# A preLN graph layer on one Trainium2 core: 46 chunks of edges taken as columns out of a table in SBUF, in place of 18 chunks loaded by single rows

## The chip, the core and the metric

The kernel runs on one core of one Trainium2 chip. The metric is the device time in microseconds (us) of one execution. Of the core's engines, TensorE (PE in the profile) does the matrix products and the transposes, VectorE (DVE) the elementwise work on masks and means, ScalarE (ACT) the activations and the copies out of PSUM, GpSimd (POOL) issues the indirect gathers, and SyncE (SP) issues the other DMAs of the main loop. Each engine works through its own list of instructions in order, and waits on semaphores for the others.

## The reference

12,500 nodes with 128 features, and 200,000 edges sorted by their target `dst`. What is computed:

```python
h = jnp.maximum(_layernorm(x, axis=-1), 0.0)
msgs = h[src]
agg = jax.ops.segment_sum(msgs, dst, num_segments=n)
deg = jax.ops.segment_sum(jnp.ones(E), dst, num_segments=n)
agg = agg / jnp.maximum(deg, 1.0)[:, None]
h0 = jax.nn.relu(agg @ Wg + h @ Ws + bg)      # 128 -> 128
h1 = jnp.tanh(h0 @ W1 + b1)                   # 128 -> 512
h2 = jnp.tanh(h1 @ W2 + b2)                   # 512 -> 512
out = x + h2 @ W3 + b3                        # 512 -> 128
```

Everything is float32.

## The kernel before

**Stage one** normalizes x in pieces of up to 14 tiles of 128 rows (L225 to L243), and stores the result h as a table `htab` of 512-byte rows in HBM. The same stage loads `src` and `dst`, turns them with PE, and keeps them as one column per chunk (`scol`, `dloc`).

**The edges** are cut into 1563 chunks of 128. A chunk needs a tile `rows` with 128 rows of h, one per edge, on 128 partitions. A one-hot mask `oh` (edges by target nodes of a window of 144) stands on the other side, and one matmul, `rows` as weights and the mask as moving data, adds the chunk's messages to `agg` in PSUM, features on partitions (`add`, L418). There are three ways to get the rows:

- 80 "raw" chunks (10 groups of 8, one group every 40 chunks from chunk 256) are gathered from x itself during stage one, by POOL (L147), and normalized in the main loop.
- 18 "slow" chunks (from chunk 160 on, every 73rd that is not raw; L96 to L104) are loaded by `row_loads` (L321) on SP's queue: 32 row numbers at a time go from SBUF into registers (a TENSOR_LOAD, L327), and each row is then a DMA of its own, whose address is a register.
- The other 1465 are gathered by POOL with one indirect DMA each (`gather`, L312). `rows_in` has `AHEAD` = 40 buffers, so the gather of a chunk waits for the matmul of the chunk 40 gathers earlier.

**The nodes** are cut into blocks of 512 (23 of them, then smaller ones). When the chunks of a block are done, the layers follow: `mean` (DVE), `part0` to `part4` (matmuls with an activation on ACT after each). These are generators; up to chunk 1312 (`QUICK`) the loop takes one step of them every second chunk, so that PE does layers between chunks, and from chunk 1312 on a small planner in the loop (`there`, `go_on`) decides. `part0` needs h of the block's own nodes, turned: `own` (L473) loads four tiles of `htab` into `hb`, `own_turned` (L482) transposes them on PE into `pt`, and ACT copies them to `hT`, one block of 512 every 64 chunks.

**Order.** The instructions of PE, the activations and copies on ACT that go through the class `act`, and the DMAs of `sp_dma` are kept in program order. The rest is placed by the framework's scheduler. `onehot(g + 2)` (L363) writes the mask of a group of 8 chunks two groups ahead, into one of `OHS` = 4 buffers.

Of the kernel before, what the change touches and what calls it, by code (L numbers as in the profile page):

```python
# [31 lines left out]
P = 128  # L32
EPS = 1e-5
CPR = 16
BLK = 512
PIECE = 14
GRP = 8
NRAW = 10
RAW0 = 256
STEP = 40  # L40
AHEAD = 40
LATE = 12
LEAD = 16
QUICK = 1312
SLOW0 = 160
EACH = 72
TOGETHER = 4
# [12 lines left out]
def windowed(ctx, tc, x, src, dst, Wg, Ws, bg, W1, b1, W2, b2, W3, b3, out, flag):  # L60
# [34 lines left out]

    slow, n = [], 0  # L96
    for c in range(SLOW0, NCH - 12):
        if raw(c):
            continue
        if n <= 0:  # L100
            slow.append(c)
            n = EACH
        else:
            n -= 1  # L104

# [11 lines left out]
    rows_in = ctx.enter_context(tc.tile_pool(name="rows_in", bufs=AHEAD))  # L117
    rows_one = ctx.enter_context(tc.tile_pool(name="rows_one", bufs=4))
    ps_c = ctx.enter_context(tc.tile_pool(name="ps_c", bufs=1, space=PSUM))
# [46 lines left out]

    htab = dram.tile([NP, D], F32, name="htab")
    scol = const.tile([P, NCOL], I32, name="scol")
    dloc = const.tile([P, NCOL], F32, name="dloc")

# [5 lines left out]
    def centre(pool, xt, k, stats, bufs=2):  # L176
        nc.vector.tensor_reduce(stats[:, 0], xt, AX.X, ALU.add)  # L177
        nc.vector.scalar_tensor_tensor(xt, spread(stats[:, 0], k), -1.0 / D, xt, op0=ALU.mult, op1=ALU.add)
        sq = pool.tile([P, k, D], F32, name=f"sq{k}", bufs=bufs)
# [13 lines left out]
    with tc.tile_pool(name="setup", bufs=1) as sp, tc.tile_pool(name="ln", bufs=2) as ln:  # L193

        def indices(name, a, pad, keep):
            r = sp.tile([NROW, ROW], I32, name="idx_raw")

            nc.vector.memset(r, pad)
            even = FULL // 16 * 16
            for s0, s1 in ((0, even), (even, FULL)):  # L200
                if s1 > s0:
                    nc.scalar.dma_start(r[s0:s1, :], a[s0 * ROW : s1 * ROW].rearrange("(p e) -> p e", e=ROW))
            nc.scalar.dma_start(r[FULL : FULL + 1, :REST], a[FULL * ROW : E].rearrange("(p e) -> p e", p=1))
            rf = sp.tile([NROW, ROW], F32, name="idx_f")
# [21 lines left out]
        for i, (t0, k) in enumerate(pieces):  # L226
# [13 lines left out]
            factors(stats)  # L240
            h = ln.tile([P, PIECE, D], F32, name="h")
# [40 lines left out]
    nc.scalar.dma_start(b3c, b3.rearrange("(p o) -> p o", o=1))  # L282
    ROWB = 4 * D
    hbytes = htab.rearrange("n d -> (n d)").bitcast(U8)
    at_i = const.tile([len(slow), P], I32, name="at_i")
# [34 lines left out]

    def row_loads():  # L321
        for i, c in enumerate(slow):
            r = rows_one.tile([P, D], F32, name="srows")
            rows_t[c] = r
            rb = r.bitcast(U8)
            for p0 in range(0, P, LOADS):
                loads, vs = nc.values_load_multi_w_load_instructions(  # L327
                    place[i : i + 1, p0 : p0 + LOADS], engines=[mybir.EngineType.SP], min_val=0,
                    max_val=(N - 1) * ROWB,
                    skip_runtime_bounds_check_because="src holds rows of x, as the indirect DMAs take it to",  # L330
                )
                for ld in loads:
                    tc.keep_in_program_order(ld)
                for p, v in enumerate(vs, p0):
                    sp_dma(rb[p : p + 1, :], hbytes[bass.ds(v, ROWB)].rearrange("(o b) -> o b", o=1))
                    if (p + 1) % TOGETHER == 0:
                        yield


# [18 lines left out]

    OHS = 4
    oh_bufs = [const.tile([P, GRP, WINDOWS[0][1]], F32, name=f"oh{i}") for i in range(OHS)]  # L360
    counts = {}

    def onehot(g):  # L363
        k = min(GRP, NCH - g * GRP)
        lo, w = window(g * GRP)
        is_raw = raw(g * GRP)
        oh = ed.tile([P, GRP, W_RAW], F32, name="ohr", bufs=2) if is_raw else oh_bufs[g % OHS]
        nc.vector.tensor_tensor(  # L368
# [28 lines left out]
    def count(b):  # L397

        n, m = blocks[b]
        dg = flat(ps_m.tile([P, 4, P], F32, name="pm"))  # L400
        pe.matmul(dg[:, :m], ones, counts.pop(b)[:, :m], start=True, stop=True)
        rd = ml.tile([P, BLK], F32, name="rd", bufs=3)
# [67 lines left out]

    owns, hTs, xss, stores = {}, {}, {}, []

    def own(s):  # L473

        n0 = s * BLK
        n = min(BLK, N - n0)
        k = -(-n // P)
        hb = ml.tile([P, BLK // P, D], F32, name="hb", bufs=3)
        sp_dma(hb[:, :k], htab[n0 : n0 + k * P, :].rearrange("(t p) d -> p t d", p=P))
        owns[s] = hb  # L480

    def own_turned(s):  # L482

        k = -(-min(BLK, N - s * BLK) // P)
        hb = owns.pop(s)
        pt = ps_t.tile([P, BLK // P, P], F32, name="pt")
        for t in range(k):
            pe.transpose(pt[:, t, :], hb[:, t, :], ident)
        hT = ml.tile([P, BLK], F32, name="hT", bufs=3)
        act.copy(hT[:, : k * P], pt[:, :k, :].rearrange("p t n -> p (t n)"))  # L490
        hTs[s] = hT

# [26 lines left out]
    def mean(b):  # L519
        n, mm, hop = costs(b)  # L520
        yield 0, 0
        mTs[b] = ml.tile([P, BLK], F32, name="mT")
        merged(b, mTs[b])

    def part0(b):
        n, mm, hop = costs(b)
        s, off = divmod(blocks[b][0], BLK)
        yield mm, 0
        p0 = flat(ps_m.tile([P, 4, P], F32, name="pm"))
        pe.matmul(p0[:, :n], ws, hTs[s][:, off : off + n], start=True, stop=False)  # L530
        yield mm, n / 90
        pe.matmul(p0[:, :n], wg, mTs.pop(b)[:, :n], start=False, stop=True)
        h0s[b] = ml.tile([P, BLK], F32, name="h0")
        act.activation(h0s[b][:, :n], p0[:, :n], AF.Relu, bias=bgc)
# [75 lines left out]

    order = [c for c in range(NCH) if not raw(c) and c not in slow]
    loading = row_loads()
    work, done, nxt, behind = [], 0, 0, 0
    ngrp = -(-NCH // GRP)
    span = BLK // per
    now = at = 0
# [9 lines left out]
    def go_on(w):  # L626
        nonlocal now
        if w:
# [3 lines left out]
            if w[1] is None:  # L632
                work.remove(w)

    own(0)
    own(1)
    own(2)
    own_turned(0)
    onehot(0)
    onehot(1)  # L640
    counted = 0
    for c in range(NCH):
# [3 lines left out]
        if c % GRP == 0 and g + 2 < ngrp:  # L646
            onehot(g + 2)
            if raw((g + 2) * GRP):
                raw_scaled(((g + 2) * GRP - RAW0) // STEP)
            if 2 <= g < 2 + NRAW:  # L650
# [10 lines left out]
        if not raw(c) and c not in slow:  # L661
            behind += 1
            batch = behind * P // (EACH * TOGETHER)
            if behind > SLOW0 - 3 * EACH and batch > (behind - 1) * P // (EACH * TOGETHER):
                next(loading, 0)
        if c >= QUICK:

            there = 7.5 + 1.251 * (NRAW * GRP + order.index(c)) if c not in slow else 0
            while soonest() and max(now, soonest()[2]) < there:
# [403 lines left out]
```

## Time and profile before

| | |
|---|---|
| median of 3 runs | 1958.97 us (1958.91 to 1960.45) |
| time of the profiled execution | 1958.05 us |
| its span, first to last instruction | 1954.9 us |
| granted TensorE clock, mean | 0.895 |
| busy: PE, DVE, ACT, POOL | 1361.4, 1108.8, 219.0, 1465.8 us |
| indirect DMAs on POOL | 80 from x, 1465 from `htab` |
| rows as single DMAs on SP's queue | 2304 (18 x 128) |

How to read it: a line of a view names the line of the kernel, the engine, the operation, what it writes and reads (out<-in), the count, the busy time with the mean of one, and the idle time of the engine just before, with what ended it. "issue" is idle time in which the engine waited for nothing that the profile shows. SPq, ACTq and POOLq are an engine's sequencer: DMAs that it issues, register instructions and waits. These don't count as busy. A line like "x24" in the timeline is a run of 24 records of one group. An fp32 matmul leaves two records, so one chunk is two.

### The profile page before, as it was taken

The page shows a single profiled execution, that of the slowest core. Times are in us where ns is not written, and L with a number is a line of the kernel's source. Part 1 is how long each engine was busy: PE and PEld are TensorE (multiplying, and loading weights), DVE is VectorE, ACT ScalarE, POOL GpSimd, SP SyncE. Part 2 cuts the span into 40 slices and gives each one's busy share as a digit, 9 for nine tenths or more (in the row PEclk, how much of TensorE's full clock was granted, in tenths as well). Part 3 has the DMA queues.
Part 4 walks back from the last instruction along what each step waited for, and adds up shares of the span by engine and source line. Part 5 has one row for each costly group of instructions (what it writes and reads, how often), then busy time and mean ns, then how long its engine had stood idle before and what let it go on. Part 6 is the DMA issues. An engine that isn't in the chain of part 4 may idle for free.

```text
span 1954.9 us, 20999 instructions
## 1 busy us (share of the span) xinstructions
PE 1361.4 (70%) x4838; PEld 796.5 (41%) x4838; DVE 1108.8 (57%) x2650; ACT 219.0 (11%) x352; POOL 1465.8 (75%) x1553
## 2 busy tenths in 40 slices
PE   0056547777788877777766766766767678888797
PEld 0034334444444444444333333433333334454466
DVE  6874867548667667645456455454554544654541
ACT  1100010011111011101101011010110101011022
POOL 7777777777777777777777777777777777777775
PEclk9999958798989898987989989889899898788698
DMA  8822222222222222222222222222222223222221
GB/s 212 233 62 59 62 54 65 53 58 65 70 59 65 70 70 59 65 70 59 65 71 70 54 71 61 62 64 59 71 54 71 70 54 83 59 66 71 63 61 44
DMA packets 124143, 139.41 MB, mean 71 GB/s; under 512 B 32776, under 2 KB 98454, under 8 KB 123816
## 3 DMA queue, kind: packets, MB, share of 16 engines
q0 software_dynamic: 49440, 101.35, 20.6%
q1 hardware_dynamic: 71374, 33.32, 6.2%
q10 hardware_dynamic: 3196, 3.32, 0.7%
q8 instruction: 40, 0.66, 0.1%
q14 instruction: 93, 0.76, 0.1%
HBM read 125.06 MB, written 12.82 MB: 71 GB/s over the span
## 4 chain that ended last, share of the span: by engine, by line
DMA 30%; issue 29%; PE 28%; POOL 7%; DVE 5%; ACT 1%; SPq 0%; ACTq 0%; POOLq 0%; DVEq 0%
DMA rows<-htab,scol 27%; PE pm L301 16%; PE agg L301 9%; POOL rows L314 7%; PE edge L301 2%; DMA xt<-in_x_dram 2%; DVE deg L384 1%; PE pt L304 1%; DVE oh L368 1%; DMA at_i<-in_src_dram 0%; ACT h L344 0%; DVE h L191 0%; DVE agg L184 0%; DVE agg L177 0%; DVE sq L183 0%
## 5 line engine op out<-in xcount | busy, mean ns | idle before, releaser
L314 POOL DMA_INDIRECT rows<-htab,scol x1465 | 1388.2, 948 | 446.7 <-issue 272.3
L301 PE MATMUL agg<-oh,rows 128*128 128x144 f32 (+3 forms) x2098 | 551.6, 366 | 321.0 <-DMA rows<-htab,scol 292.7
L301 PEld LDWEIGHTS agg<-oh,rows 128*128 128x128 f32 x2098 | 392.1, 227 | 686.1 <-DMA rows<-htab,scol 527.2
L301 PE MATMUL pm<-h,w 128*128 128x512 f32 (+4 forms) x1344 | 653.8, 585 | 15.9 <-ACT h L344 15.8
L384 DVE SCALAR_TENSOR_TENSOR deg<-shared,dloc,deg 128x144 bf16<-128x144 f32 (+17 forms) x1921 | 567.0, 326 | 29.1
L368 DVE TENSOR_TENSOR oh<-shared,dloc 128x1152 f32<-128x1152 f32 (+2 forms) x186 | 245.5, 1320 | 446.1 <-PE agg L301 304.7
L301 PE MATMUL edge<-oh,rows 128*128 128x144 f32 (+2 forms) x832 | 215.1, 349 | 129.4 <-DMA rows<-htab,scol 129.1
L301 PEld LDWEIGHTS edge<-oh,rows 128*128 128x128 f32 x832 | 141.5, 208 | 286.5 <-DMA rows<-htab,scol 221.5
L301 PEld LDWEIGHTS pm<-h,w 128*128 128x128 f32 x1344 | 227.4, 209 | 34.0 <-ACT h L344 18.1
L344 ACT ACTIVATE h<-pm,b2c 128x512 f32<-128x512 f32 (+4 forms) x112 | 70.8, 632 | 678.9 <-PE pm L301 678.9
L403 DVE TENSOR_SCALAR rd<-pm 128x512 f32<-128x512 f32 (+4 forms) x28 | 17.4, 622 | 178.5 <-PE pm L301 178.5
L344 ACT ACTIVATE h<-pm,b1c 128x512 f32<-128x512 f32 (+4 forms) x112 | 70.4, 632 | 241.1 <-PE pm L301 240.5
L147 POOL DMA_INDIRECT raw<-in_x_dram,rsrc x80 | 76.7, 959 | 25.6 <-issue 23.8
L405 DVE RECIPROCAL rd<-rd 128x512 f32<-128x512 f32 (+4 forms) x28 | 81.8, 2920 | 0.0
L467 DVE TENSOR_TENSOR mT<-agg,sums 128x136 f32<-128x136 f32 (+6 forms) x57 | 15.3, 268 | 106.2 <-PE agg L301 105.5
L209 PE MATMUL pm<-ident,idx_f 98*128 98x98 f32 x32 | 6.0, 374 | 69.2 <-DVE idx_f L205 59.1
L347 ACT COPY hT<-pt 128x512 f32<-128x512 f32 (+1 forms) x25 | 14.4, 577 | 316.2 <-PE pt L304 304.3
L304 PE MATMUL pt<-ident,hb 128*128 128x128 f32 x98 | 17.3, 305 | 45.9 <-DMA hb<-htab 22.1
L344 ACT ACTIVATE h<-pm,bgc 128x512 f32<-128x512 f32 (+4 forms) x28 | 17.7, 632 | 158.5 <-PE pm L301 158.5
L209 PEld LDWEIGHTS pm<-ident,idx_f 98*128 98x128 f32 x32 | 5.1, 224 | 69.7 <-DVE idx_f L205 30.8
L304 PEld LDWEIGHTS pt<-ident,hb 128*128 128x128 f32 x98 | 13.0, 157 | 47.3 <-issue 47.3
L585 DVE TENSOR_TENSOR o<-pt,xb 128x512 f32<-128x512 f32 x23 | 15.5, 676 | 26.7 <-PE pt L304 26.6
(71 smaller groups left out, 468.5 us busy)
## 6 DMA issues: line engine op xcount, KB each, us to landing
srows<-htab SPq DMA_DIRECT2D x2304, 0.5 KB
rows<-htab,scol POOLq DMA_INDIRECT x1465
hb<-htab SPq DMA_DIRECT2D x24, 256.0 KB
xb<-in_x_dram SPq DMA_DIRECT2D x23, 256.0 KB
out_dram<-o SPq DMA_DIRECT2D x23, 256.0 KB
htab<-h SPq DMA_DIRECT2D x6, 896.0 KB
xt<-in_x_dram SPq DMA_DIRECT2D x5, 896.0 KB
raw<-in_x_dram,rsrc POOLq DMA_INDIRECT x80
```

Of the source, the lines that this page charges most:

```text
L147: nc.gpsimd.indirect_dma_start(out=t[:, j, :], out_offset=None, in_=x, in_offset=bass.IndirectOffsetOnAxis(ap=rsrc[:, g, j : j + 1], axis=0),)
L301: tc.keep_in_program_order(nc.tensor.matmul(*a, **k))
L304: tc.keep_in_program_order(nc.tensor.transpose(*a, **k))
L314: nc.gpsimd.indirect_dma_start(out=r, out_offset=None, in_=htab, in_offset=bass.IndirectOffsetOnAxis(ap=scol[:, c : c + 1], axis=0),)
L344: tc.keep_in_program_order(nc.scalar.activation(*a, **k))
L347: tc.keep_in_program_order(nc.scalar.copy(*a))
L368: nc.vector.tensor_tensor(oh[:, :k, :w], lane[:, None, :w].to_broadcast([P, k, w]), dloc[:, g * GRP : g * GRP + k][:, :, None].to_broadcas ...
L384: nc.vector.scalar_tensor_tensor(d, lane[:, a0 - lo : a1 - lo], dloc[:, c : c + 1], d, op0=ALU.is_equal, op1=ALU.add)
L403: nc.vector.tensor_scalar(rd[:, :m], dg[:, :m], 1.0, None, op0=ALU.max)
L405: nc.vector.reciprocal(rd[:, :m], rd[:, :m])
L467: nc.vector.tensor_tensor(out, s, t, op=ALU.add)
L585: nc.vector.tensor_tensor(o[:, :whole], po[:, :whole], xb[:, :whole], op=ALU.add)
```

## The change

A table `tab` of 128 partitions by 12,544 nodes (features on partitions, 50 KB on each) is kept in SBUF: `own_turned` now copies every turned block there, and all 25 blocks of `htab` are loaded and turned in the first 100 chunks, one every 4 chunks (before: one every 64). `part0` reads the block's own h from `tab`, and `hT` is gone.

46 chunks (the words of the change say 48; the rule in the code, with 152 candidates and three in ten, gives 46), between 155 and 1435, get their rows from `tab`: ACT loads 32 numbers into registers at a time, and copies for each edge the column of its source into a tile `cols` (128 partitions by 4 bytes per copy). `turn` transposes the 128 x 128 tile on PE into a `pm` buffer of PSUM, and ACT copies it to `turned`, from where `add` takes it. The copies are handed out in batches of four, `MARGIN` = 18 gathers ahead of the chunk's use, and spread evenly over the stretch from one such chunk to the next; `turn` comes 9 gathers ahead.

No chunk is loaded by single rows any more (`lanes[0]` is empty), nor by DVE (`lanes[2]`). The 18 small DMAs of `at_i` on ACT's queue are gone; two tiles `places` are made of the loaded `src` by DVE instead.

To make room: `AHEAD` 40 to 22, pieces of stage one of up to 11 tiles in place of 14, three mask buffers in place of four, one `ohr`, `mT` and `h0` in place of two, two `rd` in place of three, and `hb` shares the two buffers of `xb`.

```diff
-PIECE = 14
+PIECE = 11
-AHEAD = 40
+AHEAD = 22
-SLOW0 = 160
-EACH = 72
+EVERY = 8
+AT = 3
+LANES = "A--A--A---"
+FROM, UNTIL = 152, 1450
+SBUFS = 4
+MARGIN = 18
...
+    lanes = ([], [], [])
+    for i, c in enumerate(c for c in range(AT, NCH, EVERY) if FROM <= c < UNTIL and not raw(c)):
+        kind = LANES[i % len(LANES)]
+        if kind != "-":
+            lanes["SAV".index(kind)].append(c)
+    apart = sum(lanes, [])
...
+    tab = const.tile([P, NP], F32, name="tab")
+    places = [const.tile([NROW, CPR // EVERY, P], I32, name=f"place{i}") for i in range(2)]
...
+            if name == "src":
+                some = r.rearrange("r (q p) -> r q p", p=P)[:, AT::EVERY]
+                for to, step in zip(places, (ROWB, 4)):
+                    nc.vector.tensor_scalar(to, some, float(step), None, op0=ALU.mult)
...
-    for i, c in enumerate(slow):
-        nc.scalar.dma_start(at_i[i : i + 1, :], src[c * P : (c + 1) * P].rearrange("(o p) -> o p", o=1))
-    place = const.tile([len(slow), P], I32, name="place")
-    nc.vector.tensor_scalar(place, at_i, float(ROWB), None, op0=ALU.mult)
+    tbytes = tab.bitcast(U8)
...
+    def offsets(lane, c, p0):
+        step = ROWB if lane == 0 else 4
+        r, q = divmod(c, CPR)
+        kind = (mybir.EngineType.SP, mybir.EngineType.Activation, mybir.EngineType.DVE)[lane]
+        loads, vs = nc.values_load_multi_w_load_instructions(
+            places[min(lane, 1)][r : r + 1, q // EVERY, p0 : p0 + LOADS], engines=[kind], min_val=0, max_val=(N - 1) * step,
...
+    def column_copies(lane):
+        copy = nc.scalar.copy if lane == 1 else nc.vector.tensor_copy
+        for c in lanes[lane]:
+            t = ed.tile([P, P], F32, name=f"cols{lane}", bufs=2)
+            columns[c] = t
+            tb = t.bitcast(U8)
+            for p0 in range(0, P, LOADS):
+                for p, v in offsets(lane, c, p0):
+                    tc.keep_in_program_order(copy(tb[:, 4 * p : 4 * p + 4], tbytes[:, bass.ds(v, 4)]))
+                    if (p + 1) % (TOGETHER if lane == 1 else LOADS) == 0:
+                        yield
+
+    def turn(c):
+        pt = ps_m.tile([P, 4, P], F32, name="pm")
+        pe.transpose(pt[:, 0, :], columns.pop(c), ident)
+        r = ed.tile([P, D], F32, name="turned", bufs=3)
+        act.copy(r, pt[:, 0, :])
+        rows_t[c] = r
...
-    OHS = 4
+    OHS = 3
...
-        hb = ml.tile([P, BLK // P, D], F32, name="hb", bufs=3)
+        hb = ml.tile([P, BLK // P, D], F32, name="xb")
...
-        hT = ml.tile([P, BLK], F32, name="hT", bufs=3)
-        act.copy(hT[:, : k * P], pt[:, :k, :].rearrange("p t n -> p (t n)"))
+        act.copy(tab[:, s * BLK : s * BLK + k * P], pt[:, :k, :].rearrange("p t n -> p (t n)"))
...
+    def load_times(lane):
+        use = [sum(o < c for o in order) for c in lanes[lane]]
...
+        step = (use[-1] - use[0]) // max(1, len(use) - 1)
+        use = [max(FROM - 46 + MARGIN, use[0] - step), *use] if lane else [use[0] - step * k for k in range(SBUFS - 1, 0, -1)] + use
+        some = LOADS if lane == 2 else TOGETHER
+        for i in range(len(lanes[lane])):
+            for k in range(P // some):
+                yield max(1, use[i] + (use[i + 1] - use[i]) * k * some // P - (0, MARGIN, MARGIN + GRP)[lane])
...
+    turns = sorted((max(1, sum(o < c for o in order) - MARGIN // 2), c) for c in sum(lanes[1:], []))
...
+            for rows_of_lane, times in loading[:2]:
+                while times and times[0] <= behind:
+                    times.pop(0)
+                    next(rows_of_lane, 0)
+            while turns and turns[0][0] <= behind:
+                turn(turns.pop(0)[1])
...
-        if c % span == span // 2 and (c // span + 1) * BLK < N:
-            own_turned(c // span + 1)
-            if (c // span + 3) * BLK < N:
-                own(c // span + 3)
+        if c % 4 == 2 and c // 4 + 1 < nown:
+            own_turned(c // 4 + 1)
+            if c // 4 + 3 < nown:
+                own(c // 4 + 3)
```

More of the change, by code (lines that the diff above doesn't have):

```diff
@@ L94, in window @@
         return per * c + first(w), w
[L96 to L104, printed above, removed]
+    lanes = ([], [], [])
[4 more added lines that the diff above has]
+    apart = sum(lanes, [])
     blocks, n = [], 0
@@ L117, in windowed @@
     rows_in = ctx.enter_context(tc.tile_pool(name="rows_in", bufs=AHEAD))
-    rows_one = ctx.enter_context(tc.tile_pool(name="rows_one", bufs=4))
+    rows_one = ctx.enter_context(tc.tile_pool(name="rows_one", bufs=SBUFS))
     ps_c = ctx.enter_context(tc.tile_pool(name="ps_c", bufs=1, space=PSUM))
@@ L167, in windowed @@
     htab = dram.tile([NP, D], F32, name="htab")
+    tab = const.tile([P, NP], F32, name="tab")
     scol = const.tile([P, NCOL], I32, name="scol")
+    ROWB = 4 * D
+    places = [const.tile([NROW, CPR // EVERY, P], I32, name=f"place{i}") for i in range(2)]
     dloc = const.tile([P, NCOL], F32, name="dloc")
@@ L178, in centre @@
         nc.vector.scalar_tensor_tensor(xt, spread(stats[:, 0], k), -1.0 / D, xt, op0=ALU.mult, op1=ALU.add)
-        sq = pool.tile([P, k, D], F32, name=f"sq{k}", bufs=bufs)
+        sq = (pool.tile([P, PIECE, D], F32, name="sq") if bufs > 1 else pool.tile([P, GRP, W_RAW], F32, name="ohr", bufs=1)[:, :, :D])[:, :k]
         if bufs > 1:
@@ L240, in windowed @@
             factors(stats)
-            h = ln.tile([P, PIECE, D], F32, name="h")
+            h = ln.tile([P, PIECE, D], F32, name="h", bufs=2)
             scale(h[:, :k], xt, k, stats)
@@ L282, in windowed @@
     nc.scalar.dma_start(b3c, b3.rearrange("(p o) -> p o", o=1))
-    ROWB = 4 * D
     hbytes = htab.rearrange("n d -> (n d)").bitcast(U8)
-    at_i = const.tile([len(slow), P], I32, name="at_i")
-    for i, c in enumerate(slow):
-        nc.scalar.dma_start(at_i[i : i + 1, :], src[c * P : (c + 1) * P].rearrange("(o p) -> o p", o=1))
-    place = const.tile([len(slow), P], I32, name="place")
-    nc.vector.tensor_scalar(place, at_i, float(ROWB), None, op0=ALU.mult)
+    tbytes = tab.bitcast(U8)
     total = const.tile([1, len(blocks)], F32, name="total")
@@ L318, in gather, with row_loads @@
         rows_t[c] = r
-    def row_loads():
-        for i, c in enumerate(slow):
+    def offsets(lane, c, p0):
[4 more added lines that the diff above has]
+            places[min(lane, 1)][r : r + 1, q // EVERY, p0 : p0 + LOADS], engines=[kind], min_val=0, max_val=(N - 1) * step,
+            skip_runtime_bounds_check_because="src holds rows of x, as the indirect DMAs take it to",
+        )
+        for ld in loads:
+            tc.keep_in_program_order(ld)
+        return enumerate(vs, p0)
+    def row_loads(lane):
+        for c in lanes[lane]:
             r = rows_one.tile([P, D], F32, name="srows")
@@ L326, in row_loads @@
             for p0 in range(0, P, LOADS):
[L327 to L334, printed above, removed]
+                for p, v in offsets(lane, c, p0):
                     sp_dma(rb[p : p + 1, :], hbytes[bass.ds(v, ROWB)].rearrange("(o b) -> o b", o=1))
@@ L337, in row_loads @@
                         yield
+    columns = {}
+    def column_copies(lane):
+        copy = nc.scalar.copy if lane == 1 else nc.vector.tensor_copy
+        for c in lanes[lane]:
+            t = ed.tile([P, P], F32, name=f"cols{lane}", bufs=2)
+            columns[c] = t
+            tb = t.bitcast(U8)
+            for p0 in range(0, P, LOADS):
+                for p, v in offsets(lane, c, p0):
+                    tc.keep_in_program_order(copy(tb[:, 4 * p : 4 * p + 4], tbytes[:, bass.ds(v, 4)]))
[7 more added lines that the diff above has]
+        rows_t[c] = r
     class act:
@@ L366, in onehot @@
         is_raw = raw(g * GRP)
-        oh = ed.tile([P, GRP, W_RAW], F32, name="ohr", bufs=2) if is_raw else oh_bufs[g % OHS]
+        oh = ed.tile([P, GRP, W_RAW], F32, name="ohr", bufs=1) if is_raw else oh_bufs[g % OHS]
         nc.vector.tensor_tensor(
@@ L401, in count @@
         pe.matmul(dg[:, :m], ones, counts.pop(b)[:, :m], start=True, stop=True)
-        rd = ml.tile([P, BLK], F32, name="rd", bufs=3)
+        rd = ml.tile([P, BLK], F32, name="rd", bufs=2)
         nc.vector.tensor_scalar(rd[:, :m], dg[:, :m], 1.0, None, op0=ALU.max)
@@ L469, in merged @@
             nc.vector.tensor_tensor(out, s, rd[:, a0 - n : a1 - n], op=ALU.mult)
-    owns, hTs, xss, stores = {}, {}, {}, []
+    owns, xss, stores = {}, {}, []
     def own(s):
         n0 = s * BLK
-        n = min(BLK, N - n0)
-        k = -(-n // P)
-        hb = ml.tile([P, BLK // P, D], F32, name="hb", bufs=3)
+        k = -(-min(BLK, N - n0) // P)
+        hb = ml.tile([P, BLK // P, D], F32, name="xb")
         sp_dma(hb[:, :k], htab[n0 : n0 + k * P, :].rearrange("(t p) d -> p t d", p=P))
@@ L488, in own_turned @@
             pe.transpose(pt[:, t, :], hb[:, t, :], ident)
-        hT = ml.tile([P, BLK], F32, name="hT", bufs=3)
-        act.copy(hT[:, : k * P], pt[:, :k, :].rearrange("p t n -> p (t n)"))
-        hTs[s] = hT
+        act.copy(tab[:, s * BLK : s * BLK + k * P], pt[:, :k, :].rearrange("p t n -> p (t n)"))
     def own_part(b):
@@ L521, in mean @@
         yield 0, 0
-        mTs[b] = ml.tile([P, BLK], F32, name="mT")
+        mTs[b] = ml.tile([P, BLK], F32, name="mT", bufs=1)
         merged(b, mTs[b])
@@ L526, in part0 @@
         n, mm, hop = costs(b)
-        s, off = divmod(blocks[b][0], BLK)
+        n0 = blocks[b][0]
         yield mm, 0
         p0 = flat(ps_m.tile([P, 4, P], F32, name="pm"))
-        pe.matmul(p0[:, :n], ws, hTs[s][:, off : off + n], start=True, stop=False)
+        pe.matmul(p0[:, :n], ws, tab[:, n0 : n0 + n], start=True, stop=False)
         yield mm, n / 90
         pe.matmul(p0[:, :n], wg, mTs.pop(b)[:, :n], start=False, stop=True)
-        h0s[b] = ml.tile([P, BLK], F32, name="h0")
+        h0s[b] = ml.tile([P, BLK], F32, name="h0", bufs=1)
         act.activation(h0s[b][:, :n], p0[:, :n], AF.Relu, bias=bgc)
@@ L609, in layers @@
         )
-    order = [c for c in range(NCH) if not raw(c) and c not in slow]
-    loading = row_loads()
+    order = [c for c in range(NCH) if not raw(c) and c not in apart]
+    def load_times(lane):
+        use = [sum(o < c for o in order) for c in lanes[lane]]
+        if not use:
+            return
+        step = (use[-1] - use[0]) // max(1, len(use) - 1)
[4 more added lines that the diff above has]
+                yield max(1, use[i] + (use[i + 1] - use[i]) * k * some // P - (0, MARGIN, MARGIN + GRP)[lane])
+    loading = [
+        (column_copies(i) if i else row_loads(0), list(load_times(i))) for i in range(len(lanes))
+    ]
+    turns = sorted((max(1, sum(o < c for o in order) - MARGIN // 2), c) for c in sum(lanes[1:], []))
     work, done, nxt, behind = [], 0, 0, 0
     ngrp = -(-NCH // GRP)
-    span = BLK // per
     now = at = 0
@@ L633, in go_on @@
                 work.remove(w)
+    nown = -(-N // BLK)
     own(0)
     own(1)
+    own_turned(0)
     own(2)
-    own_turned(0)
     onehot(0)
@@ L649, in windowed @@
                 raw_scaled(((g + 2) * GRP - RAW0) // STEP)
+            copies, times = loading[2]
+            while times and times[0] <= behind:
+                times.pop(0)
+                next(copies, 0)
             if 2 <= g < 2 + NRAW:
@@ L660, in windowed @@
             nxt += 1
-        if not raw(c) and c not in slow:
+        if not raw(c) and c not in apart:
             behind += 1
-            batch = behind * P // (EACH * TOGETHER)
-            if behind > SLOW0 - 3 * EACH and batch > (behind - 1) * P // (EACH * TOGETHER):
-                next(loading, 0)
+            for rows_of_lane, times in loading[:2]:
+                while times and times[0] <= behind:
+                    times.pop(0)
+                    next(rows_of_lane, 0)
+            while turns and turns[0][0] <= behind:
+                turn(turns.pop(0)[1])
         if c >= QUICK:
-            there = 7.5 + 1.251 * (NRAW * GRP + order.index(c)) if c not in slow else 0
+            there = 7.5 + 1.251 * (NRAW * GRP + order.index(c)) if c not in apart else 0
             while soonest() and max(now, soonest()[2]) < there:
```

## The prediction

> **What bounds the kernel now.** I read the page first (span, engines, costliest groups), then the waits of POOL, then the timeline of stage one, then the stretches in which PE was behind. From the page:
>
> ```profile
> span 1954.9 us, 20999 instructions
> ...
> PE 1361.4 (70%) x4838; PEld 796.5 (41%) x4838; DVE 1108.8 (57%) x2650; ACT 219.0 (11%) x352; POOL 1465.8 (75%) x1553
> ...
> L314 POOL DMA_INDIRECT rows<-htab,scol x1465 | 1388.2, 948 | 446.7 <-issue 272.3
> ```
>
> POOL looks 75% busy, but its idle time is all of one kind. From the waits of POOL, and the instructions of line 314 (count; shortest, median, longest; first and last start):
>
> ```profile
> POOL rows L314 <- issue: 272.3, 893, 0.3
> POOL rows L314 <- PE agg L301: 79.0, 259, 0.3
> ...
> L314 POOL DMA_INDIRECT rows<-htab,scol x1465: 940/944/2081, 104.2 to 1937.8; - x184
> ```
>
> The last column of the waits is the longest one: 0.3 us, whoever is named, so the 0.3 us is the fixed gap between two gathers and no gather ever waited for a buffer. The first starts at 104.2, the last at 1937.8: 1833.6 us for 1464 steps, **1.2525 us a gather**. POOL sets the pace from start to end; 17 us of tail come after it. A gather less is worth 1.2525 us, as long as nothing else takes over.
>
> **The change part by part.**
>
> *Gathers.* 1563 chunks less 80 raw less 46 leaves 1437 gathers against 1465: 28 x 1.2525 = **35.1 us less**. (With the 48 of the change's words it would be 2.5 us more; the rule gives 46.) The tail has no chunk from the table after 1435 and stays.
>
> *Start of the gathers.* Timeline of stage one, all engines:
>
> ```profile
> 38.36 0.25 ACT L187 ACTIVATE agg<-agg,eps 128x14 f32<-128x14 f32 x1 [5.96 <-DMA at_i<-in_src_dram]
> ...
> 93.78 1.82 SPq L310 DMA_DIRECT2D hb<-htab  x3
> ...
> 97.25 1.09 PE L304 MATMUL pt<-ident,hb 128*128 128x128 f32 x4 [22.11 <-DMA hb<-htab]
> ...
> 102.91 0.95 POOL L147 DMA_INDIRECT raw<-in_x_dram,rsrc  x1 [0.30 <-issue]
> 104.16 0.94 POOL L314 DMA_INDIRECT rows<-htab,scol  x1 [0.30 <-DVE deg L384]
> ...
> 106.78 0.71 PE L301 MATMUL agg<-oh,rows 128*128 128x76 f32 x2 [8.44 <-DMA rows<-htab,scol]
> ```
>
> The table in HBM is complete at 93.78, when `hb` may read it; POOL is busy with raw chunks until 104.16. So stage one may grow by 10.4 us for nothing. Two more pieces and two small DVE multiplications cost it a little (a few fixed costs of some 0.25 us); the `at_i` DMAs that go had held up ACT's normalization (the 5.96 us of the first row is one such hold). I take 0, bounds 0 to +10.
>
> *The table.* 25 loads of 256 KB and 25 blocks of four transposes move into the first 100 chunks (125 us). Three loads issued together at 93.78 let PE start at 97.25, 3.5 us; in the change each has two blocks' time, 10 us. Bandwidth and transposes:
>
> ```profile
> 50.00:100.00 50.00, 4.20 (x20) 3.25 (x20) 43.35 (x52) 8.37 (x9) 38.12 (x40) 1.00 0.84 228
> 100.00:150.00 50.00, 27.80 (x73) 17.84 (x73) 40.12 (x73) 0.58 (x1) 37.81 (x41) 1.00 0.23 59
> ...
> L304 PE MATMUL pt<-ident,hb 128*128 128x128 f32 x98 | 17.3, 305 | 45.9 <-DMA hb<-htab 22.1
> ```
>
> (Last columns: clock, DMA share, GB/s.) 6.4 MB in 125 us is 51 GB/s beside 59, with 228 shown possible. 4 x 0.305 = 1.2 us of PE per 5 us, while PE is busy 27.8 of 50 us: it fits. Cost 0. The 46 `turn` transposes are 46 x 0.305 = 14 us of PE, under its 30% of idle time: 0.
>
> *ScalarE.* This decides. A chunk costs ACT 128 copies, four register loads and one copy of 128 x 128. Nothing in the trace is a copy of one column at a register's address, so it is bounded. Instructions of SP's row loads, the flag's loads, and SP's timeline:
>
> ```profile
> L310 SPq MOVE srows<-htab x2304: 29/29/29, 97.8 to 1764.1; - x192
> L310 SPq DMA_DIRECT2D srows<-htab x2304: 227/228/345, 97.8 to 1764.2; - x192
> ...
> L327 SPq TENSOR_LOAD <-place x72: 2057/2154/2722, 95.7 to 1715.6; - x72
> ...
> L1038 SPq TENSOR_LOAD <-flag x1: 447/447/447, 1933.7 to 1933.7; - x1
> ...
> L1038 ACTq TENSOR_LOAD <-flag x1: 465/465/465, 1948.8 to 1948.8; - x1
> ...
> 312.84 3.84 SPq L310 DMA_DIRECT2D srows<-htab  x12
> ```
>
> 32 numbers load in 2.15 us on SP, and a load of one costs ACT what it costs SP: 4 x 2.15 = 8.6 us a chunk. 67 ns a number is what the row says; the Trainium skill ("Runtime: NRT & Kernel Launch", Instruction fetch mechanics) gives about 200 ns a register for its loads, by which a chunk's loads were 25.6 us and ScalarE would be overrun; this trace's row disagrees and decides. One register instruction goes with each row; SP's step of 3.84/12 = 0.32 us is 0.228 + 0.029 and twice 0.03 for handing over, so the register instruction is worth 0.06. The copy itself, by forms on ACT, and ACT's timeline:
>
> ```profile
> L347 ACT COPY hT<-pt 128x512 f32<-128x512 f32 x24 | 14.1, 586 | 315.4 <-PE pt L304 303.5 <-DMA hb<-htab 12.0
> ...
> L347 ACT COPY sums<-edge 128x128 f32<-128x128 f32 x1 | 0.3, 265 | 0.6 <-PE edge L301 0.6
> ...
> 258.50 1.84 ACT L344 ACTIVATE h<-pm,b1c 128x512 f32<-128x512 f32 x3
> ```
>
> 586 and 265 ns at 512 and 128 columns: 0.836 ns a column and 158 ns fixed, so 161 ns for 4 bytes. Three activations of 0.69 us in 1.84 us step by 0.575: consecutive ones overlap by 0.11, which leaves a step of 0.05 to 0.06 for the small copy. **Lower end 0.06 us a copy** (overlap, register work hidden), **upper end 0.22** (161 ns without overlap and 0.06 for the register in a row). I take **0.12**: overlapped copies, as the row of three shows, with the register instruction in a row.
>
> What else ACT does, by forms:
>
> ```profile
> L344 ACT ACTIVATE h<-pm,b2c 128x512 f32<-128x512 f32 x92 | 63.2, 687 | 657.3 <-PE pm L301 657.3
> L344 ACT ACTIVATE h<-pm,b1c 128x512 f32<-128x512 f32 x92 | 63.0, 687 | 234.4 <-PE pm L301 234.4
> L344 ACT ACTIVATE h<-pm,bgc 128x512 f32<-128x512 f32 x23 | 15.8, 687 | 141.7 <-PE pm L301 141.7
> L344 ACT ACTIVATE h<-pm,b3c 128x512 f32<-128x512 f32 x23 | 15.8, 687 | 80.1 <-PE pm L301 80.1
> ...
> L347 ACT COPY sums<-edge 128x280 f32<-128x280 f32 x21 | 8.2, 391 | 151.8 <-PE edge L301 90.9 <-DVE deg L384 60.8
> ```
>
> 166 us for 23 blocks of 64 chunks; from chunk 155 to 1435 there are 20 blocks, 144 us, 3.1 us for each of the 46 chunks, and 0.3 for the turned copy. ACT's sum per chunk: 8.6 + 128 x 0.12 + 3.4 = **27.4 us**. The time that it has: the chunks lie 23, 23 and 31 gathers apart, 25.67 on average, 32.15 us. So ACT is 85% full, and even the short stretches (28.8 us) hold it. The balance tips at (32.15 - 3.4 - 8.6)/128 = **0.157 us a copy**. Below it the copies cost the end nothing; their cover is the idle time of ACT between two activations. An activation waits in ACT's list behind at most the copies handed out before it (four at a time, now and then a load: 0.5 to 2.6 us), and PE behind it; below chunk 1312 PE's next step for that block comes two chunks (2.5 us) or more later, so this too is mostly covered.
>
> By the Trainium skill ("ScalarE: Activation LUTs", What ACT_TABLE_LOAD costs) an ACTIVATE with immediates takes 186 ns and 0.833 ns an element and overlaps the next by about 93 ns: an estimate of 0.096 us a copy, with which ScalarE's sum were 24.3 us, inside the limit as well.
>
> *22 buffers.* The gathers now stop when PE is some 22 chunks behind the issue, about 19 behind the landing (first row 104.16 to first matmul 106.78 is 2 gathers in flight). PE's two worst places:
>
> ```profile
> 259.24 2.07 PE L301 MATMUL pm<-h,w 128*128 128x512 f32 x2 [13.86 <-ACT h L344]
> 261.11 4.07 PE L301 MATMUL agg<-oh,rows 128*128 128x144 f32 x24
> 265.02 1.39 PE L301 MATMUL edge<-oh,rows 128*128 128x144 f32 x10
> 266.78 0.51 PE L301 MATMUL edge<-oh,rows 128*128 128x144 f32 x2 [0.37 <-DMA rows<-htab,scol]
> ...
> 1636.01 13.90 PE L301 MATMUL pm<-h,w 128*128 128x512 f32 x32
> ...
> 1654.30 5.56 PE L301 MATMUL agg<-oh,rows 128*128 128x144 f32 x44
> ...
> 1660.53 0.51 PE L301 MATMUL edge<-oh,rows 128*128 128x144 f32 x2 [0.42 <-DMA rows<-htab,scol]
> ```
>
> At 261.11 PE runs 34 records, 17 chunks, before it waits for data again at 266.78, in which time 4.5 landed: it was 12 to 13 behind. At 1654.30: 22 chunks, 5 landed, 17 behind. Both pass under 19, the second narrowly. The smaller rings make this worse by a little:
>
> ```profile
> DVE oh L368 <- PE agg L301: 304.7, 72, 10.2
> ```
>
> DVE often stands at the mask ring already; with three buffers in place of four it is one group (10 us) less ahead of PE. That can add up to 8 chunks to the early place and nothing where PE has no backlog. I charge 2 us for both places, bounds 0 and 2 x 8 x 1.25 = 20. `mT`, `h0`, `rd` and the shared `xb` are reused a block (80 us) later or, for `xb`, after the table is done: 0. The row DMAs that leave SP's queue free it: no gain, SP is on no path here.
>
> **Sum.** Profiled execution 1958.05 - 35.1 + 2 = **1925 us**; its time is 0.9 below the median of the runs and 3.15 above its span. POOL's floor without any stall is 1923.
>
> **Rivals.**
>
> *A, ScalarE becomes the bound (slower).* From 0.157 us a copy on, every chunk costs 46 x (128t + 12.0 - 32.15) more. At 0.163 that is 33 us and the gain is gone. At 0.16 (a record without overlap) it is 1943, at 0.19, the middle of 0.16 and 0.22, 46 x 4.2 = 192 us: **2115**; at 0.22 2293. PE would wait for turned columns and activations, and POOL for buffers. For it: 12,000 more instructions on one sequencer, and register-addressed copies are nowhere in the trace. Against: the overlap in the row of three. The slow load of the skill's page above would belong here too; I give it 0.01 of this chance.
>
> *B, the ring of 22 stalls POOL.* If ACT's batches or the shorter mask ring push PE 20 or more behind at several places, each costs 3 to 8 us: 5 to 25 in all, **1938**. For it: 17 of 19 at 1654. Against: elsewhere PE catches up within a few chunks.
>
> *C, stage one ends more than 10 us later*: up to 10 us, **1933**. Against: the `at_i` holds go.
>
> **How the numbers follow.** Forecast 0.47 (own range 1919 to 1935); A 0.36; B 0.13; C 0.04. Runs of this kernel differ by 0.08%, so no change is within 0.2% (4 us). A is faster below 0.163 (0.03), the same just there (0.02), slower above (0.31); B is faster 0.11, same 0.01, slower 0.01; C 0.03 and 0.01. Faster 0.64, same 0.04, slower 0.32. The range goes from 1919 to 2030, which A reaches at 0.175 us a copy; that leaves out half of A.
>
> **What would show it.** POOL: 1437 gathers from about 104 to 1903, with waits of 0.3 us only; a wait of microseconds there for PE is B, a later first gather C. ACT: the step of column copies in a run (0.12 or less right, 0.16 or more A), TENSOR_LOAD near 2.15 us, and ACT idle time left. PE waiting at `pm<-cols` for ACT would mean A.

## The result, and the profile after

| | before | after |
|---|---|---|
| median | 1959.71 us (1958.91 to 1961.53, 4 runs) | 1925.85 us (1923.71 to 1927.21, 4 runs) |
| profiled execution: time, span | 1958.05, 1954.9 us | 1926.09, 1924.3 us |
| indirect DMAs from `htab` | 1465 | 1437 |

The ratio is 0.9825, with a 95% interval of 0.9808 to 0.9842. The forecast was 1925 us. In the last four experiments below (e9 to e12) the kernel before itself, measured beside them, took 2327 to 2348 us in place of 1957 to 1964, for a cause that was not found.

The page of the kernel after, its span, engines, and two of its costliest groups:

```profile
span 1924.3 us, 28354 instructions
...
PE 1352.3 (70%) x4884; PEld 797.0 (41%) x4884; DVE 1117.9 (58%) x2661; ACT 806.7 (42%) x6290; POOL 1440.2 (75%) x1525
...
L316 POOL DMA_INDIRECT rows<-htab,scol x1437 | 1362.2, 948 | 437.9 <-issue 265.1
...
L356 ACT COPY cols<-tab 128x4 uint8 x5888 | 603.6, 190 | 290.5 <-issue 286.1
```

PE, DVE and POOL are as busy as before; ACT went from 219 to 807 us of busy time. The waits of POOL and the instructions of the gathers' line show whether POOL still runs without a pause:

```profile
POOL rows L316 <- issue: 265.1, 870, 0.3
POOL rows L316 <- DMA rows<-htab,scol: 71.0, 233, 0.3
POOL rows L316 <- PE agg L303: 55.1, 181, 0.3
...
L316 POOL DMA_INDIRECT rows<-htab,scol x1437: 940/944/1927, 104.7 to 1903.5; - x180
```

The longest wait is again the fixed 0.3 us. 1798.8 us for 1436 steps are 1.2526 us a gather, as before (1.2525). The start of the gathers, in the timeline of all engines:

```profile
93.45 18.18 SPq L312 DMA_DIRECT2D xb<-htab  x4
...
104.69 0.94 POOL L316 DMA_INDIRECT rows<-htab,scol  x1 [0.30 <-issue]
```

The table in HBM is complete at 93.45 (before: 93.78), and the first gather comes at 104.69 (104.16). What ACT does now, from the instructions of the copies' and the loads' lines, ACT's waits and its timeline:

```profile
L356 ACTq ALU_OP  x5888: 35/35/48, 265.2 to 1722.5; - x197
L356 ACT COPY cols<-tab x5888: 177/189/203, 265.3 to 1723.1; 128x4 uint8 x197
...
L327 ACTq TENSOR_LOAD <-place x184: 1943/2006/2489, 262.9 to 1713.4; - x184
...
ACT cols L356 <- issue: 286.1, 193, 2.1
...
818.30 1.61 ACT L356 COPY cols<-tab 128x4 uint8 x16
821.16 3.31 ACT L356 COPY cols<-tab 128x4 uint8 x32 [1.25 <-issue]
826.30 1.24 ACT L356 COPY cols<-tab 128x4 uint8 x12 [1.84 <-issue]
832.57 0.27 ACT L375 COPY turned<-pm 128x128 f32<-128x128 f32 x1 [5.03 <-PE pm L306]
```

One copy lasts 0.19 us, but 32 of them take 3.31: the step is (3.31 - 0.19)/31 = 0.101 us, so each overlaps the one before by 0.09. The register load shows as idle time of 1.2 to 1.9 us ahead of a batch, less than its own 2.0 us, because copies handed out before the load are still running; all such idle time is 286 us for 184 loads, 1.55 each. The 5.03 us before `turned` are idle time in which ACT waits for PE: room to spare.

### The profile page after: what moved, and what is told of

Read it like the earlier page. It is cut to its first block, busy times and chain, and to the rows that moved or that the text cites. A ratio compares the mean times of both kernels' runs of the same rounds, so it can differ in the third digit from the quotient of the medians.

```text
span 1924.3 us, 28354 instructions
## 1 busy us (share of the span) xinstructions
PE 1352.3 (70%) x4884; PEld 797.0 (41%) x4884; DVE 1117.9 (58%) x2661; ACT 806.7 (42%) x6290; POOL 1440.2 (75%) x1525
## 3 DMA queue, kind: packets, MB, share of 16 engines
q10 hardware_dynamic: 3160, 3.31, 0.6%
## 4 chain that ended last, share of the span: by engine, by line
DMA 32%; issue 28%; PE 24%; POOL 11%; DVE 4%; ACT 0%; POOLq 0%; DVEq 0%; ACTq 0%
DMA rows<-htab,scol 32%; PE pm L303 14%; PE agg L303 7%; POOL rows L316 7%; POOL raw L148 4%; PE edge L303 2%; DVE deg L412 1%; PE pt L306 1%; DVE oh L396 1%; DVE rd L433 0%; ACT h L372 0%; DVE shared L181 0%; DVE shared L188 0%; DVE raw L182 0%; DVE ohr L187 0%
## 5 line engine op out<-in xcount | busy, mean ns | idle before, releaser
L316 POOL DMA_INDIRECT rows<-htab,scol x1437 | 1362.2, 948 | 437.9 <-issue 265.1
L303 PE MATMUL agg<-oh,rows 128*128 128x144 f32 (+3 forms) x2046 | 538.1, 363 | 321.8 <-DMA rows<-htab,scol 297.5
L356 ACT COPY cols<-tab 128x4 uint8 x5888 | 603.6, 190 | 290.5 <-issue 286.1
L303 PE MATMUL pm<-h,w 128*128 128x512 f32 (+4 forms) x1344 | 645.6, 578 | 23.0 <-ACT h L372 15.7
L303 PEld LDWEIGHTS agg<-oh,rows 128*128 128x128 f32 x2046 | 375.0, 225 | 665.6 <-DMA rows<-htab,scol 530.6
L303 PE MATMUL edge<-oh,rows 128*128 128x144 f32 (+2 forms) x828 | 211.2, 346 | 125.9 <-DMA rows<-htab,scol 124.2
L375 ACT COPY tab<-pt 128x512 f32<-128x512 f32 (+1 forms) x25 | 14.4, 577 | 130.8 <-PE pt L306 130.8
L372 ACT ACTIVATE h<-pm,b3c 128x512 f32<-128x512 f32 (+4 forms) x28 | 17.7, 633 | 87.7 <-PE pm L303 87.7
L306 PE MATMUL pt<-ident,xb 128*128 128x128 f32 x98 | 25.8, 417 | 13.6 <-DMA xb<-htab 13.6
```

The source lines that it names most:

```text
L303: tc.keep_in_program_order(nc.tensor.matmul(*a, **k))
L306: tc.keep_in_program_order(nc.tensor.transpose(*a, **k))
L316: nc.gpsimd.indirect_dma_start(out=r, out_offset=None, in_=htab, in_offset=bass.IndirectOffsetOnAxis(ap=scol[:, c : c + 1], axis=0),)
L356: tc.keep_in_program_order(copy(tb[:, 4 * p : 4 * p + 4], tbytes[:, bass.ds(v, 4)]))
L372: tc.keep_in_program_order(nc.scalar.activation(*a, **k))
L375: tc.keep_in_program_order(nc.scalar.copy(*a))
```

## The experiments

All start from the changed kernel. What follows from each stands right behind it.

**e1, e2, e3: how many chunks go by columns.** One line is changed:

```diff
-LANES = "A--A--A---"
+LANES = "-"              # e1: no chunk, 1483 gathers
+LANES = "A-A--"          # e2: 61 chunks, 1422 gathers
+LANES = "A-"             # e3: 76 chunks, 1407 gathers
```

> No chunk from the table, all else of the change kept (early table, rings, pieces): 1483 gathers, 46 more. Theory (POOL's rate is the whole price, nothing else of the change costs or gains): 1925.9 + 46 x 1.2525 = 1983.5 us, within 4. Rival (ScalarE's batches and the turns also cost PE time that reaches the end): less than 1975. Rival (the early table and the smaller rings gain or cost by themselves): more than 1990 or, against before, 18 gathers more than before is not +22.5 us.

> Two candidates in five by column copies: 61 chunks, 1422 gathers. Theory (a chunk costs ScalarE 128 x 0.10 + 4 x 1.4 + 2.4 + 0.3 = 21.1 us, and it has 19 gathers or 23.8 us): it still fits, 1925.9 - 15 x 1.2525 = 1907 us. Rival (ScalarE at 85 per cent as forecast from 0.12 us a copy, 26.3 us needed of 23.8): ScalarE becomes the bound, 61 x 2.5 = 150 us more, 2060.

> Every second candidate: 76 chunks, 1407 gathers, 15 gathers or 18.8 us apart. Theory: ScalarE needs 128 x 0.10 + 4 x 1.4 + 1.9 + 0.3 = 20.7 us a chunk and is the bound: 1888 + 76 x 1.9 = 2030 us, ScalarE without idle time between the copies from chunk 155 on, and gathers that wait for PE. Rival (POOL stays the bound): 1888 us.

Measured: e1 1983.21 us (ratio to before 1.0116, interval 1.0099 to 1.0133), e2 1906.77 us (0.9729, 0.9713 to 0.9745), e3 2007.8 us (1.0244, 1.0219 to 1.0268); the kernel before, measured beside these and e4, took 1960.61. From no chunk to 46 to 61 the time falls by 57.4 and 19.1 us, for 46 and 15 gathers: 1.25 and 1.27 us a gather. e2's rival, 2060 us, falls. The rest of the change costs and gains nothing that shows in these medians: e1 has 18 gathers more than the kernel before, worth 22.5 us, and lies 22.6 above it, with an interval of some 3 us to either side.

With 76 chunks it turns. The waits of e3, its copies' line, and all waits of ACT between 270 and 1750 us (the last two rows):

```profile
POOL rows L316 <- PE agg L303: 160.9, 228, 5.8
PEld pm L303 <- ACT h L372: 153.0, 55, 14.2
...
PEld pm L306 <- ACT h L372: 132.6, 31, 7.2
...
POOL rows L316 <- PE pm L306: 29.4, 14, 25.5
...
L356 ACT COPY cols<-tab x9728: 176/189/210, 265.0 to 1829.1; 128x4 uint8 x199
...
ACT cols L356 <- issue: 420.3, 305, 2.5
ACT h L372 <- PE pm L303: 12.4, 8, 4.9
```

The chain is the one that the prediction's first rival described: PE waits for activations that stand behind copies on ACT, and POOL waits for buffers that PE has not emptied (now up to 25.5 us). In those 1480 us ACT waits 12.4 us for PE; the other 420 us are the idle time ahead of batches, as with the register loads of the change, 1.4 us each. So ScalarE is the bound, and 1564 us for 76 chunks are **20.6 us of ScalarE a chunk**; the chunks lie 15 gathers, 18.8 us, apart. The expectation's 20.7 held. Its time was 22 us too high. Some 9 of these are the 20.58 in place of 20.7; the others fit the head start that the copies and the ring have, which the expectation left out, but no run separates that.

**e4, e9, e11: what one copy costs.** Each column twice, at the same place (e4), or the second time into a tile that nobody reads (e9, and e11 once more):

```diff
                 for p, v in offsets(lane, c, p0):
-                    tc.keep_in_program_order(copy(tb[:, 4 * p : 4 * p + 4], tbytes[:, bass.ds(v, 4)]))
+                    for _ in range(2):                                                                       # e4
+                        tc.keep_in_program_order(copy(tb[:, 4 * p : 4 * p + 4], tbytes[:, bass.ds(v, 4)]))
...
+                    tc.keep_in_program_order(copy(tb[:, 4 * p : 4 * p + 4], tbytes[:, bass.ds(v, 4)]))       # e9, e11
+                    tc.keep_in_program_order(copy(ub[:, 4 * p : 4 * p + 4], tbytes[:, bass.ds(v, 4)]))
```

> Every column copied twice (the same column to the same place), 1437 gathers as in the change. Theory: ScalarE needs 256 x 0.10 + 4 x 1.4 + 3.4 = 34.6 us a chunk and has 32.15: 46 x 2.5 = 113 us more, 2040 us. Rival (ScalarE has more room than that, or PE's waits count instead): no more than 20 us above the change.

Measured: 2853.1 us (1.4556, 1.4527 to 1.4585), 800 us more than expected. ACT's timeline (the first two rows are cut so narrow that each holds two copies) and the copies' line of e4:

```profile
342.41 0.41 ACT L357 COPY cols<-tab 128x4 uint8 x2
342.63 0.29 ACT L357 COPY cols<-tab 128x4 uint8 x2
...
801.81 1.47 ACT L357 COPY cols<-tab 128x4 uint8 x9
...
L357 ACT COPY cols<-tab x11776: 180/193/201, 264.8 to 2676.7; 128x4 uint8 x200
```

The copies are no longer 0.10 us apart but (1.47 - 0.19)/8 = 0.16 on average. The records of the single instructions show why: the first copy of each pair raises a semaphore and the second waits for it, since both write the same bytes. The pair takes 0.32 us: the second copy starts 0.22 after the first (0.41 less its own 0.19), and the next pair 0.10 after that (0.29 less 0.19). 128 x 0.32 + 4 x 2.0 + 3.4 = 52.4 us a chunk; the row gives (2676.7 - 264.8)/46 = 52.4. The edit did not double the cost in question, it added a wait, and I had not foreseen that. What it measured is **0.22 us for a copy that waits for the one before it**: the figure of the prediction's upper end, but by another sum, 0.19 of the copy and 0.03 until the next one starts, where the prediction added 0.16 and 0.06 for the register.

> Every column copied twice, the second time into a tile of its own that nobody reads, so that no copy waits for another; 1437 gathers. Theory (a copy without a wait steps 0.10 us whatever it writes): 256 x 0.10 + 4 x 1.4 + 3.4 = 34.6 us a chunk against 32.15, 46 x 2.5 = 113 us less the 16 us of lead that the run with 76 chunks showed: 2025 us, within 20. Rival (the double number of copies, not the wait among them, made the other doubled run long): near 2850 us.

> The run of the doubled copies into a second tile once more, since on the chip of its first run the kernel before took 2341 us in place of 1960. Theory (a copy without a wait steps 0.10 us): 34.6 us a chunk against 32.15, 2025 us, within 20. Rival (the doubled number of copies, not the wait among them, makes it long): near 2850 us.

Measured: e9 2890.46 us beside 2340.92 of the kernel before (1.2366, 1.2319 to 1.2414), e11 2898.18 beside 2334.53 (1.2410, 1.2340 to 1.2481). With such a time of the kernel before, neither theory nor rival can be held against these totals. The step of the copies can be read all the same. ACT's timeline of e9, ACT's two largest entries in its waits, and the register instructions of the second copies:

```profile
800.59 0.20 ACT L357 COPY cols<-tab 128x4 uint8 x1
800.68 0.20 ACT L358 COPY again<-tab 128x4 uint8 x1
800.78 0.20 ACT L357 COPY cols<-tab 128x4 uint8 x1
800.87 0.20 ACT L358 COPY again<-tab 128x4 uint8 x1
...
ACT cols L357 <- issue: 603.7, 738, 2.7
ACT again L358 <- issue: 338.5, 554, 1.9
...
L358 ACTq ALU_OP  x5888: 2/35/1405, 303.9 to 2672.1; - x197
```

Where they run, the doubled copies without a wait step by 0.095 us, against 0.16 with it: so it is the wait and not their number that made e4's copies slow. But ACT stands idle 1292 times for "issue" here, 942 us, where the change had 193 such pauses for 184 loads. Part of it shows in the last row: a register instruction, 48 ns at the longest in the change, now takes up to 1405 ns. Why, and what e9 would take otherwise, stays open.

**e5: the ring.**

```diff
-AHEAD = 22
+AHEAD = 12
```

> 12 gathers ahead in place of 22, all else as in the change. Theory (the ring counts only where PE falls behind by more than it holds; in the change's trace that is 17 chunks at 1622 us and 13.5 at 263 us, elsewhere under 5, and 2 are in flight): POOL waits about 7 gathers, 9 us, at the late place and 3 to 4, 4 us, at the early one, 1939 us, and nowhere else. Rival (the ring works all along, against jitter of the landings and ScalarE's batches): waits of POOL spread over the run and more than 1950 us.

Measured: 1941.89 us (0.9908, 0.9891 to 0.9925), 16.0 above the change. POOL's waits in e5:

```profile
POOL rows L316 <- DMA rows<-htab,scol: 207.5, 681, 0.3
POOL rows L316 <- issue: 174.0, 571, 0.3
POOL rows L316 <- PE agg L303: 31.3, 86, 5.3
...
POOL rows L316 <- PE pm L306: 11.5, 7, 9.7
...
264.39 0.94 POOL L316 DMA_INDIRECT rows<-htab,scol  x1 [5.35 <-PE agg L303]
...
1627.79 0.94 POOL L316 DMA_INDIRECT rows<-htab,scol  x1 [9.71 <-PE pm L306]
```

There are two waits over 0.3 us in the whole run, 5.35 us at 264 and 9.71 us at 1628 (the last two rows, from POOL's timeline): the two places where PE is behind, 5.0 and 9.4 us beyond the fixed gap where 4 and 9 were expected from the backlogs of 13.5 and 17 chunks. They are 14.4 of the 16.0 us. The rival, a ring that works all along, falls.

**e6, e7, e8: other ways beside it.** Fifteen chunks by single rows on SP's queue again (e6), the same with 61 chunks by columns (e7), fifteen by DVE's column copies (e8):

```diff
-LANES = "A--A--A---"
+LANES = "A--A-SA---"     # e6: 1422 gathers
+LANES = "A-A-SA-A--"     # e7: 1407 gathers
+LANES = "A--A-VA---"     # e8: 1422 gathers
```

> 46 chunks by columns and 15 by single rows on SP's queue again: 1422 gathers. Theory (POOL's rate is the price, the two ways share nothing but the DMA engines, which are 23 per cent busy): 1925.9 - 15 x 1.2525 = 1907 us, as with 61 chunks by columns. Rival (row DMAs slow the gathers or hold up SP's other loads): more than 1915 us.

> 61 chunks by columns and 15 by single rows: 1407 gathers, as many as with 76 by columns. Theory: ScalarE has 18.75 gathers, 23.5 us, and needs 21.1; POOL stays the bound: 1888 us. Rival (ScalarE at 90 per cent with stretches of 15 gathers, 18.8 us, makes PE wait and the 22 buffers no longer cover it): 1895 to 1920 us, with waits of POOL over 1 us.

> 46 chunks by ScalarE's column copies and 15 by the same copies on DVE: 1422 gathers. Theory if DVE's copies overlap as ScalarE's do (0.07 us a step for its smallest operations, 4 loads of 2.2 us: 18 us a chunk in a batch of four, every 100 us): 1907 us. Rival (a batch of 32 copies with its load, 5 us, in front of a mask makes PE wait for oh, and DVE has no overlap): 1910 to 1940 us.

Measured: e6 1909.40 us (0.9744, 0.9727 to 0.9760), **e7 1888.01 us (0.9632, 0.9616 to 0.9648)**, e8 1906.92 us (0.9729, 0.9709 to 0.9748); the kernel before, beside these and e5, 1959.80. All three lie on the line of 1.25 us a gather; e6 2 us above it. No wait of POOL is longer than the fixed 0.3 us in any of them, so the three rivals fall. e7 is the fastest kernel measured, 38 us below the change, with the same 1407 gathers at which e3 failed: there ScalarE had 18.8 us a chunk, here 23.5 for the 20.6 that it needs. POOL's first entry in the waits of e7, and the timeline of DVE in e8:

```profile
POOL rows L316 <- DMA rows<-htab,scol: 199.7, 655, 0.3
...
806.37 3.47 DVE L356 COPY cols<-tab 128x4 uint8 x32 [1.96 <-issue]
809.74 0.68 DVE L431 TENSOR_SCALAR rd<-pm 128x512 f32<-128x512 f32 x1
...
814.20 1.28 DVE L396 TENSOR_TENSOR oh<-shared,dloc 128x1152 f32<-128x1152 f32 x1
```

DVE's copies step by 0.106 us, no better than ScalarE's and not the 0.07 that I had expected, and a batch of 32 with its load holds DVE for 5.4 us; the mask behind it was still in time.

**e10, e12: all three ways at once**, with one buffer less for room:

```diff
-AHEAD = 22
+AHEAD = 21
-LANES = "A--A--A---"
+LANES = "A-AVSA-A--"     # 61 by ScalarE, 15 by DVE, 15 by rows: 1392 gathers
```

> 61 chunks by ScalarE's columns, 15 by DVE's and 15 by single rows, 21 gathers ahead (one buffer less, for room): 1392 gathers. Theory: POOL is still the bound, 1925.9 - 45 x 1.2525 = 1869.5 us. Rival (DVE at 70 per cent and ScalarE at 90 hold PE up, and the ring no longer covers it): 1875 to 1900 us, with waits of POOL over 1 us.

> The run with three ways once more, for the same reason: 61 chunks by ScalarE's columns, 15 by DVE's, 15 by single rows, 21 gathers ahead, 1392 gathers. Theory: POOL is still the bound, 1869.5 us. Rival: DVE and ScalarE hold PE up and the ring of 21 no longer covers it, 1875 to 1900 us, with waits of POOL over 1 us.

Measured: e10 2522.94 us beside 2340.92 of the kernel before (1.0793, 1.0723 to 1.0864), e12 2529.23 beside 2334.53 (1.0844, 1.0794 to 1.0894). As with e9 and e11, the 1869.5 us were neither reached nor refuted. Two entries of e12's waits:

```profile
ACT cols L356 <- issue: 924.3, 1150, 2.6
...
ACT h L372 <- PE pm L303: 72.0, 54, 5.5
```

As in e9, ACT pauses for "issue" far more often (1150 times) than it has loads (244). A kernel with 40,122 instructions lost there to one with 20,999. The cause was not found. That more instructions lose more is only a guess, and their number alone does not give the time: e9, with 40,124, took 2890 us.

## Why the prediction was right, point by point

- *POOL sets the pace, 1.2525 us a gather.* Right. The step is 1.2526 after, and e1, e2, e7 and e8 lie within 1 us of 1925.85 plus 1.2525 us for each gather more or less.
- *35.1 us less.* In the profiled executions the gathers' stretch went from 1833.6 to 1798.8 us, 34.8 less. Of it 0.5 is given back at the start (104.69 for 104.16) and 3.7 in the tail: the last gather starts 20.8 us before the end of the span, before 17.1. Outside the span it is 1.4 us less (time less span: 3.15 before, 1.8 after). So the 2 us that were charged for the ring of 22 did not arise there (POOL never waited); the tail, which was taken as unchanged, cost about as much. Two small errors cancelled, which was luck. One reason for the longer tail is the clock. PE's last layers in its timeline, and their stretch with the granted clock in the third column from the end, after:

```profile
1910.08 7.47 PE L303 MATMUL pm<-h,w 128*128 128x100 f32 x48 [0.49 <-ACT h L372]
...
1910.10:1917.50 7.40, 7.40 (x48) 7.12 (x48) 0.00 (x0) 2.54 (x8) 0.00 (x0) 0.77 0.01 2
```

  and before:

```profile
1942.88 5.85 PE L301 MATMUL pm<-h,w 128*128 128x100 f32 x48 [0.43 <-ACT h L344]
...
1942.90:1948.70 5.80, 5.80 (x48) 5.50 (x48) 0.00 (x0) 2.53 (x8) 0.00 (x0) 1.00 0.00 0
```

  and in e7:

```profile
1875.37 5.85 PE L303 MATMUL pm<-h,w 128*128 128x100 f32 x48 [0.49 <-ACT h L372]
...
1875.40:1881.20 5.80, 5.80 (x48) 5.50 (x48) 0.00 (x0) 2.53 (x8) 0.00 (x0) 1.00 0.00 0
```

  The same 48 records took 7.47 us at a granted clock of 0.77, and 5.85 at 1.00, before and in e7. That is 1.6 of the 3.7 us, and belongs to this one execution. The rest does not go with the clock: with these records at 5.85 us, the tail is still 19.5 us in e7, 20.0 to 20.3 in e8, e1 and e2 and 20.9 in e5 (e6: 18.0), against 17.1 in the one profiled execution of the kernel before. e1 has it without a chunk from the table, so it would come with another part of the change; which one was not tested.
- *Stage one does not reach the gathers.* Right: the table is complete 0.3 us sooner, in spite of two more pieces.
- *The early table costs nothing.* Right, by e1. Loads landed after 3.2 us in the median, of the 10 us that each had.
- *A copy costs 0.12 us, bounds 0.06 and 0.22.* Right in kind, and close to the 0.10 measured partly by luck, since both of its terms were off and the errors nearly cancelled. The copy alone was put at a step of 0.05 to 0.06; it lasts 0.19 us in place of 0.16, overlaps by 0.09 in place of 0.11, and so steps 0.10. The register instruction was put in a row with it at 0.06; it adds nothing. It is an ALU_OP of 35 ns on the sequencer, which runs beside the engine: the last one starts 0.6 us ahead of its copy (1722.5 and 1723.1 in the rows of line 356). A step of 0.22 does occur, as e4 shows, where a copy waits for the one before it, and the prediction had no row that excluded it: the row of three overlapping activations was the right one to choose by, since like them the copies don't wait for each other.
- *ScalarE is 85% full, 27.4 us a chunk.* Mis-sized on the safe side: 128 x 0.101 + 4 x 1.55 + 3.4 = 22.5 us, or 20.6 when it is packed (e3), that is 64 to 70% of 32.15 us. The sum counted a load at its full 2.15 us; a load takes 2.0 and hides some 0.5 of that behind copies in flight. That the balance tips where a chunk's sum exceeds the time between chunks was right: the 20.6 us fit into 23.5 (e7) and not into 18.8 (e3). The 0.157 us a copy at which it was to tip was not measured; with the smaller loads the same sum gives about 0.18, an estimate.
- *Rival A* did not come about in the change; e3 and e4 show that it exists, with the waits that it was said to have. *Rival B*: not with 22 buffers; with 12, at the two places named. *Rival C*: no.
- Two slips in the working change nothing: *A*'s formula gives 1940 us at 0.16 us a copy, not 1943, and 22 buffers less 2 gathers in flight are 20, not 19.

## What to carry to other kernels

When one engine sets the pace without a pause, the worth of taking work off it can be read as a fixed price per unit, and it holds until another engine's sum per unit exceeds the time between units: work out that sum for every engine that gets the work. In e7 ScalarE was filled to 20.6 of 23.5 us, 88%, and it cost nothing. A ring of buffers need only hold the largest backlog of its consumer; the backlog can be counted in the trace of the kernel before, from the run of back-to-back chunks after each stall.

Very small instructions are cheap only as long as none waits for the one before it: 0.10 us against 0.22 here. Look at whether they write different bytes before costing them by the overlapped step.

## What the runs showed of the hardware that was not expected

- A ScalarE copy of 128 x 4 bytes at a register's address lasts 0.19 us and steps 0.095 to 0.10; with a semaphore wait on its predecessor it steps 0.22. The Trainium skill ("ScalarE: Activation LUTs", What ACT_TABLE_LOAD costs) gives 186 ns and an overlap of about 93 for an ACTIVATE with immediates; the copies agree with it.
- 32 numbers load into ScalarE's registers in 2.0 us and into DVE's in 2.15, about 65 ns each.
